# Taking VectorE instructions with two SBUF operands out of an eight-layer hybrid network on one core

## The chip, the cores and the metric

The kernel runs on one core of one Trainium2 chip. Times are device microseconds of one launch; the kernel before took 1440.38 us (median of 3 runs, 1433.18 to 1441.21). The profile is one further execution, recorded by the hardware profiler.

## The reference

A sequence of T = 2048 tokens of width 128, in f32, goes through eight residual layers, each fed the layernorm of x (`x = x + f(layernorm(x))`):

```python
x = x + L0_attn_a(ln(x))   # delta rule, 16 heads of 8: state += clip(0.9 k (v - k.state)), o = clip(state q)
x = x + L0_ffn(ln(x))      # softmax router, 2 of 8 experts + a shared one
x = x + L0_attn_b(ln(x))   # rotary, 15 largest causal logits, MLP on the keys' Gram matrix, palette sampling
x = x + L0_ffn(ln(x))
x = x + L1_attn_a(ln(x))   # linear attention, 16 heads of 8
x = x + L1_ffn(ln(x))      # sigmoid router, 2 of 8 experts + a shared one
x = x + L1_attn_b(ln(x))   # decaying linear attention, 16 heads of 8
x = x + L1_ffn(ln(x))
```

The first layer is a recurrence over all tokens. The palette layer picks 15 earlier keys for each token, gathers them, runs a small MLP, turns its output into a position on a 16 x 16 palette and a softmax weight per key, and samples the palette bilinearly. The softmax router takes the two largest of eight probabilities, the sigmoid router the two largest of `scores + bias`, weighted by the plain scores.

## The kernel before

The 16 tiles of 128 tokens are cut into nine groups, `TILES = [1, 2, 2, 2, 2, 2, 2, 2, 1]`. For each group the program writes down `delta_prepare` (queries, keys, values of the first layer), `delta_chain` (the recurrence), `delta_output`, and then `layers`: softmax router and experts (`softmax_ffn`), `palette_keys`, `palette_select`, `palette_mlp`, `palette_sample`, and the later layers. Stages are named "prepare", "chain", "output", "feed 1", "keys", "select", "network", "sample", "feed 2", "linear", "feed 3", "decay", "feed 4".

Nothing of this is issued as it is written. `Recorder` (line 37) keeps every operation, works out who needs whom, and `arrange` (line 527) then places them all in one order with costs for each operation (`cost`, line 344). Where several operations could start on an engine, the one with the smallest key goes first: its place in the program less the lead of its stage and group in the table `LEADS` (line 46). All engines get their instructions from line 636, so the profile names nearly everything L636, and tiles have to tell them apart. The scheduler also counts a port that GpSimd and those VectorE instructions share that read and write SBUF alone (`port`, line 405). In gaps of TensorE it puts filler matmuls on `zeros` (line 626); they compute nothing that is used.

Buffers are shared: `tw*` hold 128 x 256 f32, `t2k*`, `t4k*` and `t8k*` are wider. Five PSUM banks (`bank`) serve everything but the chain, which has `da_state` and two `da_coef`. When the chain is over its buffers are lent to the others, so names such as `da_ke`, `da_ks`, `da_rows`, `da_outs` and `da_kb` then stand for other work.

The chain runs over 256 blocks of 8 tokens. A block has four scans on VectorE (`da_outs<-da_rows,da_coef`), after each some products into `da_rows`, a transpose (`da_dT`), a matmul into `da_state`, a mask on VectorE (`da_sm`), a matmul into `da_coef` and a subtraction into `da_rows` for the block after next; GpSimd makes `da_prod` two blocks ahead.

The places the change touches:

- `normed_T`: statistics on VectorE, `rstd` by two GpSimd instructions, then `shift = -mean * rstd` (tile `ln_nb`) by one VectorE instruction, then ScalarE applies both. It runs 72 times.
- `top2`: for 64 tiles in 36 calls, VectorE finds the eight largest of eight (`t2_mx`) and their places (`t2_ix`, in the profile `t_ix`), casts two places (`t_ixf`), compares them with 0 to 7 (`t_oh`), adds the two one-hots (`t_hot`); the caller multiplies with the weights (`ff_wd`, `mf_cf`).
- `softmax_ffn`: bias added out of PSUM into `ff_lg`, maximum, subtraction, exponential, sum, reciprocal, scaling; all but the exponential on VectorE, all in SBUF.
- `sigmoid_ffn`: ScalarE writes the scores to SBUF (`mf_sc`), VectorE adds the bias (`mf_bs`).
- `palette_keys`: four GpSimd products and two VectorE sums for the rotary embedding, a square on ScalarE, a sum and a bound on VectorE (`b_ss`).
- `palette_select`: after the largest 15 are found, three VectorE instructions make the distances `b_df`. Then 15 GpSimd gathers per tile read `b_table`.
- `palette_sample`: softmax weights (`b_wk`, `b_tot`), positions (`b_f`), differences to 0..15 in x and y (128 x 480), tents by two ScalarE instructions, one weighted tent (`b_wy`, 128 x 240), then GpSimd's four products of 960 (`t4kA`) and VectorE's sums.
- `delta_prepare`, `delta_output`, `delta_project`, `decay_attention`: a bound, a running maximum (`da_peak`), a clamp and a decay factor.

Of the kernel before, what the change touches and what calls it, by code (L numbers as in the profile page):

```python
# [18 lines left out]
P = 128  # L19
T = 2048  # L20
# [13 lines left out]
LOWEST = -3.0e38  # L34


class Recorder:
# [6 lines left out]
    FULL = 3500  # L44

    LEADS = {
        "prepare": [685, 1641, 2227, 1637, 932, 723, -140, 947, 2240],
        "chain": [3059, 2806, 2732, 2807, 2881, 2963, 2807, 2787, 3818],
        "output": [-231, -1175, 343, -231, -1136, -815, -1408, -3037, 36],
        "feed 1": [-869, -836, -732, -888, -1239, -1948, -2920, 423, 428],  # L50
        "keys": [-839, 8778, 2817, 2921, 2750, 3260, 2756, -75, 7010],
        "select": [261, -2380, -1879, -2588, -2788, -7871, -2344, -5168, -5908],
        "network": [1694, 1836, 1022, 924, 258, 711, 3372, 2137, 88],
        "sample": [6673, 4807, 6996, 2241, 409, 4927, 2879, 483, 4943],
        "feed 2": [453, -812, 880, 533, -787, 838, 1841, -5585, -2829],
        "linear": [-375, -875, -795, 500, 1267, -1260, -755, 29, -921],
        "feed 3": [317, -219, 715, 7152, 6750, -382, -1957, -1707, -769],
        "decay": [-1757, -1097, -1119, -1867, -1575, -1798, -8825, -2837, -4500],
        "feed 4": [-2273, -2252, -2310, -3252, -3143, -2535, -6364, -6239, -8229],
# [284 lines left out]
    def cost(self, op, writes, reads):  # L344
# [26 lines left out]
        if e == "ACT":  # L371
            gelu = self.table(op) == self.TABLES["Gelu"]
            busy = 0.07 + n * (1.0e-3 if gelu else 0.8e-3)
            done = busy + 0.1
            if isinstance(kw.get("scale"), (self.View, bass.AP)):
                busy, done = busy + 0.12, done + 0.12
            if isinstance(kw.get("bias"), (self.View, bass.AP)):
                done += 0.09
            return busy, done
# [66 lines left out]
    def fill(self, begin):  # L446


        if self.filler is None or self.filler["quiet"].buf["slot"] is None:
            return []  # L450
        while self.recent and self.recent[0][0] < begin - self.WINDOW:
            self.recent.pop(0)
        lack = self.FULL - sum(c for _, c in self.recent)
        out = []
        quiet, n = self.filler["quiet"], self.filler["columns"]
        while lack > 0 and len(out) < 8:
            t0, where = max(self.load_free, self.stream_end - 0.05), None
            q = quiet.buf
            if q["slot"] is not None and not self.pending and q["kind"]["to_go"]:
                t0, where = max(t0, q["end"]), quiet  # L460
            free = [s for s in self.kinds["bank"]["slots"] if s["buf"] is None and s["free"] <= begin]
            if free:
                f = min(free, key=lambda f: f["free"])
                t1 = max(self.load_free, self.stream_end - 0.05, f["free"])
                if where is None or t1 < t0:
                    t0 = t1
                    where = self.kinds["bank"]["tiles"][self.kinds["bank"]["slots"].index(f)]
            one = n / 2.4e3 / self.rate(t0)
            if where is None or t0 + one > begin + (0.15 if not out and lack > 0.25 * self.FULL else 0.0):
                break  # L470
            end = self.run(t0, 1, 0.045, n / 2.4e3, n)
            if where is not quiet:
                f["free"] = end + 0.05
            out.append((t0, where))
            lack -= n
        return out
# [163 lines left out]
def hybrid_kernel(ctx: ExitStack, tc: tile.TileContext, ins: dict, out: bass.AP):  # L640
# [84 lines left out]
    nc.gpsimd.memset(mhalf, -0.5)  # L725
    ones = keep([P, W], "ones", F32)
# [8 lines left out]
    def normed_T(g):  # L735
# [8 lines left out]
        for j in range(n):  # L744
            nc.vector.bn_aggr(out=mv[:, j, :], in_=st[:, j, :])
        nc.gpsimd.tensor_scalar(rstd, mv[:, :, 1], 1e-5, None, ALU.add)
        nc.gpsimd.tensor_tensor(rstd, rstd, mhalf[:, :n], ALU.pow)
        shift = small([P, W // P], "ln_nb")[:, :n]
        nc.vector.scalar_tensor_tensor(
            out=shift, in0=mv[:, :, 0], scalar=-1.0, in1=rstd, op0=ALU.mult, op1=ALU.mult  # L750
        )
# [48 lines left out]
    def top2(vals):  # L800
# [3 lines left out]
        ix = small([P, W // P, E], "t2_ix", U32)[:, :n]  # L804
        ixf = small([P, W // P, 2], "t2_ixf")[:, :n]
        oh = small([P, 2, W // P, E], "t2_oh")[:, :, :n]
        hot = small([P, W // P, E], "t2_hot")[:, :n]
        for j in range(n):
            nc.vector.max(out=mx[:, j, :], in_=vals[:, j, :])
            nc.vector.max_index(out=ix[:, j, :], in_max=mx[:, j, :], in_values=vals[:, j, :])  # L810
        nc.vector.tensor_copy(ixf, ix[:, :, 0:2])
        for s in range(2):
            nc.vector.tensor_tensor(
                oh[:, s],
                i8.unsqueeze(1).to_broadcast([P, n, E]),
                ixf[:, :, s : s + 1].to_broadcast([P, n, E]),
                ALU.is_equal,
            )
        nc.vector.tensor_tensor(hot, oh[:, 0], oh[:, 1], ALU.add)
        return hot  # L820

# [15 lines left out]
    peak = keep([P, 1], "da_peak")  # L844
    carry = keep([P, HD], "da_carry")
# [8 lines left out]
    nc.vector.memset(peak, 0.0)  # L854
# [54 lines left out]
    def delta_prepare(g):  # L909
# [9 lines left out]
        pa = bank("da_aps")[:, :NP]  # L919
# [3 lines left out]
        nc.scalar.activation(lo, pa, AF.Abs, scale=0.9)  # L923
        nc.vector.tensor_scalar(lo, lo, TINY, 2.0 * TINY, ALU.is_lt, ALU.mult)
# [176 lines left out]
    def delta_output(g):  # L1101
# [6 lines left out]
        pm = small([P, HD], "da_pm")  # L1108
# [17 lines left out]
        mx = small([P, 1], "da_mx")  # L1126
        nc.vector.tensor_reduce(out=mx, in_=pm, axis=AX.X, op=ALU.max)
        nc.vector.tensor_tensor(peak, peak, mx, ALU.max)
        delta_project(g, po)

    def delta_project(g, po):

        o = tw("da_o", TILES[g] * P)
        nc.vector.tensor_scalar(o, po, 0.9, -1.0, ALU.mult, ALU.max)
        nc.vector.tensor_scalar(o, o, 1.0, None, ALU.min)
# [66 lines left out]
    def softmax_ffn(g):  # L1202
# [4 lines left out]
        mx = small([P, W // P], "ff_mx")[:, :n]  # L1207
        tot = small([P, W // P], "ff_tot")[:, :n]
        nc.vector.tensor_tensor(lg, pl, w("f_gbias").unsqueeze(1).to_broadcast([P, n, E]), ALU.add)
        nc.vector.tensor_reduce(out=mx, in_=lg, axis=AX.X, op=ALU.max)  # L1210
        nc.vector.tensor_tensor(lg, lg, mx.unsqueeze(2).to_broadcast([P, n, E]), ALU.subtract)
        nc.scalar.activation(lg, lg, AF.Exp)
        nc.vector.tensor_reduce(out=tot, in_=lg, axis=AX.X, op=ALU.add)
        nc.vector.reciprocal(tot, tot)
        nc.vector.tensor_tensor(lg, lg, tot.unsqueeze(2).to_broadcast([P, n, E]), ALU.mult)
        wd = small([P, W // P, E], "ff_wd")[:, :n]
        nc.vector.tensor_tensor(wd, top2(lg), lg, ALU.mult)
# [50 lines left out]

    def palette_keys(g):
# [10 lines left out]
        for key in (False, True):  # L1280
# [10 lines left out]
            for lo, a, b, op in ((0, cs, sn, ALU.subtract), (half, sn, cs, ALU.add)):  # L1291
# [3 lines left out]
                nc.vector.tensor_tensor(r[:, :, lo : lo + half], tt[:, 0], tt[:, 1], op)  # L1295
            sq = tw("b_sq", n * P).rearrange("p (j c) -> p j c", c=P)
            nc.scalar.activation(sq, r, AF.Square)
            ss = small([P, W // P], "b_ss")[:, :n]
            nc.vector.tensor_reduce(out=ss, in_=sq, axis=AX.X, op=ALU.add)
            nc.vector.tensor_scalar(ss, ss, 1e-24, None, ALU.max)  # L1300
            nc.gpsimd.tensor_tensor(ss, ss, mhalf[:, :n], ALU.pow)
            rn = tw("b_rn", n * P).rearrange("p (j c) -> p j c", c=P)
# [12 lines left out]
    def palette_select(g, i, IT, InT):  # L1315
# [23 lines left out]
        nc.vector.tensor_copy(df, ix[:, :TOPK])  # L1339
        nc.vector.tensor_scalar(df, df, w("tpos")[:, i : i + 1], -1.0 / T, ALU.subtract, ALU.mult)  # L1340
        nc.vector.tensor_scalar(df, df, 0.0, None, ALU.max)
# [82 lines left out]
    def palette_sample(zb, xt):  # L1424
# [4 lines left out]
        nc.scalar.activation(wk, zb[:, 2, :], AF.Exp, bias=mx, scale=1.0)  # L1429
        nc.vector.tensor_reduce(out=tot, in_=wk, axis=AX.X, op=ALU.add)  # L1430
        nc.vector.reciprocal(tot, tot)
        nc.vector.tensor_scalar(wk, wk, tot, None, ALU.mult)
        f = small([P, 2, TOPK], "b_f")
        nc.scalar.activation(f, zb[:, 0:2, :], AF.Tanh)
        nc.vector.tensor_scalar(f, f, 1.0, 0.5 * (PAL - 1), ALU.add, ALU.mult)
        nc.vector.tensor_scalar(f, f, 0.0, float(PAL - 1), ALU.max, ALU.min)
# [4 lines left out]
        nc.vector.tensor_tensor(  # L1441
            hat, f.unsqueeze(2).to_broadcast(shape),
            w("i16").unsqueeze(1).unsqueeze(3).to_broadcast(shape), ALU.subtract,
# [4 lines left out]
        nc.vector.tensor_tensor(wy, hat[:, 1], wk.unsqueeze(1).to_broadcast([P, PAL, TOPK]), ALU.mult)  # L1448
# [24 lines left out]
        nc.vector.tensor_tensor(xt, xt, py, ALU.add)  # L1473
# [64 lines left out]
    def sigmoid_ffn(g):  # L1538
        xn, xnT = normed_T(g)
        nt, n = TILES[g], TILES[g] * P  # L1540
        sc = small([P, W // P, E], "mf_sc")[:, :nt]
        nc.scalar.activation(sc, router_logits("mf_l", xnT, w("m_gate")), AF.Sigmoid)
# [3 lines left out]
        nc.vector.tensor_tensor(cf, top2(bs), sc, ALU.mult)  # L1546
# [53 lines left out]
    def decay_attention(g):  # L1600
# [13 lines left out]
        nc.scalar.activation(lam, project("de_l", cs, w("d_w2")), AF.Sigmoid, bias=w("d_b2"), scale=1.0)  # L1614
        nc.scalar.activation(lam, lam, AF.Identity, bias=base, scale=fifth)
        nc.vector.tensor_scalar(lam, lam, 0.0, 0.9995, ALU.max, ALU.min)
# [68 lines left out]

    nc.vector.tensor_scalar(peak, peak, CAP - 2.01, None, ALU.is_gt)
# [134 lines left out]
```

## Time and profile before

| | us |
|---|---|
| median of the runs | 1440.38 |
| the profiled execution | 1444.89 |
| its span, first to last instruction | 1442.6 |
| busy: scans of the chain (`da_outs`) | 220.3 |
| gathers `b_table` | 208.2 + 23.8 |
| loads of ScalarE's tables (105) | 134.7 |
| filler matmuls (456 in program order) | 139.8 |

In the profile PE is TensorE's matmuls, PEld its weight loads, DVE is VectorE, ACT is ScalarE, POOL is GpSimd and SP issues DMAs. A row of a group reads: line, engine, operation, written tile <- read tiles, shapes, count | busy us, mean ns of one | idle time of the engine ahead of them and what ended it. Tiles that differ in number alone share a name. A row of a tile's own view gives the shortest, median and longest instruction in ns. A row of windows gives the window, its length, and per engine the busy us with the number of instructions, then the granted TensorE clock as a share of full speed, and the DMA share and rate.

```profile
q0 software_dynamic: 7936, 16.47, 4.5%
q1 hardware_dynamic: 30713, 10.36, 2.9%
HBM read 24.24 MB, written 3.27 MB: 19 GB/s over the span
```

DMA queues (packets, MB, share of 16 engines) : none takes more than 4.5%.

### The profile page before, as it was taken

The page shows a single profiled execution, that of the slowest core. Times are in us where ns is not written, and L with a number is a line of the kernel's source. Part 1 is how long each engine was busy: PE and PEld are TensorE (multiplying, and loading weights), DVE is VectorE, ACT ScalarE, POOL GpSimd, SP SyncE. Part 2 cuts the span into 40 slices and gives each one's busy share as a digit, 9 for nine tenths or more (in the row PEclk, how much of TensorE's full clock was granted, in tenths as well). Part 3 has the DMA queues.
Part 4 walks back from the last instruction along what each step waited for, and adds up shares of the span by engine and source line. Part 5 has one row for each costly group of instructions (what it writes and reads, how often), then busy time and mean ns, then how long its engine had stood idle before and what let it go on. Part 6 is the DMA issues. An engine that isn't in the chain of part 4 may idle for free.

```text
span 1442.6 us, 24150 instructions
## 1 busy us (share of the span) xinstructions
PE 1262.0 (87%) x7034; PEld 901.9 (63%) x7034; DVE 1127.2 (78%) x5192; ACT 818.5 (57%) x2029; POOL 871.4 (60%) x1233
## 2 busy tenths in 40 slices
PE   4898989898989999998989989898989898888886
PEld 3475667676566667775766657665766565445664
DVE  4788698987897689778997788988887766847733
ACT  4132244436553586577654846485557876576575
POOL 3226153557478657774876647676786758775723
PEclk9876697958898699789997989999889999899989
DMA  5001000001001000110001000010011001100000
GB/s 147 25 6 31 8 1 6 11 25 40 2 11 40 21 2 7 30 38 3 7 21 27 24 3 1 27 37 10 4 32 33 0 1 34 39 22 1 1 5 9
DMA packets 38791, 28.46 MB, mean 20 GB/s; under 512 B 21222, under 2 KB 34081, under 8 KB 38649
## 3 DMA queue, kind: packets, MB, share of 16 engines
q0 software_dynamic: 7936, 16.47, 4.5%
q1 hardware_dynamic: 30713, 10.36, 2.9%
q8 instruction: 58, 0.95, 0.3%
q14 instruction: 84, 0.69, 0.2%
HBM read 24.24 MB, written 3.27 MB: 19 GB/s over the span
## 4 chain that ended last, share of the span: by engine, by line
PE 40%; DVE 27%; POOL 14%; ACT 10%; issue 5%; DMA 3%; SPq 1%; POOLq 0%; DVEq 0%; ACTq 0%
PE bank L636 29%; PE da_coef L636 7%; POOL t2kA L636 5%; DVE da_rows L636 5%; DVE da_outs L636 5%; PE da_state L636 3%; ACT twS L636 3%; POOL t4kA L636 2%; DVE twD L636 2%; ACT t2kS L636 2%; DMA t2kA<-b_table,b_ix 2%; DVE t2kA L636 2%; DVE da_sm L636 2%; ACT t2kA L636 1%; POOL da_kb L636 1%
## 5 line engine op out<-in xcount | busy, mean ns | idle before, releaser
L636 POOL DMA_INDIRECT t2kA<-b_table,b_ix x215 | 208.2, 968 | 76.2 <-issue 47.0
L636 DVE TENSOR_TENSOR_SCAN da_outs<-da_rows,da_coef 128x30 f32<-128x30 f32 (+3 forms) x1024 | 220.3, 215 | 12.6
L636 DVE TENSOR_TENSOR da_rows<-da_coef,da_outs 128x16 f32<-128x16 f32 (+6 forms) x1116 | 186.7, 174 | 13.2
L636 POOL TENSOR_TENSOR da_prod<-da_kl,da_ke 128x112 f32<-128x112 f32 (+2 forms) x264 | 92.7, 371 | 163.4 <-PE da_coef L636 158.7
L636 ACT ACT_TABLE_LOAD x105 | 134.7, 1283 | 4.1 <-PE bank L636 1.7
L636 POOL TENSOR_TENSOR t4kA<-t2kA,t2kA 128x960 f32<-128x960 f32 x56 | 114.6, 2074 | 34.8 <-DVE t2kA L636 16.7
L636 PEld LDWEIGHTS da_coef<-da_kl,da_sm 128*128 128x128 f32 x508 | 93.9, 222 | 64.9 <-DVE da_sm L636 38.7
L636 PEld LDWEIGHTS da_state<-da_dT,da_kb 128*128 128x128 f32 x512 | 104.9, 225 | 41.0 <-DVE da_dT L636 22.1
L636 POOL TENSOR_TENSOR twS<-twS,twS 128x256 f32<-128x256 f32 (+1 forms) x119 | 79.8, 682 | 62.3 <-ACT de_last L636 35.7
L636 PE MATMUL da_coef<-da_prod,ones_blk 128*128 128x224 f32 x256 | 90.0, 438 | 25.4 <-DVE da_rows L636 17.5
L636 PE MATMUL da_coef<-da_kl,da_sm 128*128 128x8 f32 x508 | 97.5, 265 | 14.7 <-DVE da_sm L636 13.4
L636 PE MATMUL da_state<-da_dT,da_kb 128*128 128x32 f32 x512 | 98.4, 277 | 10.7 <-DVE da_dT L636 8.9
L636 DVE TENSOR_TENSOR da_sm<-da_state,ones_blk 128x128 f32<-128x128 f32 x254 | 70.9, 279 | 40.8 <-PE da_state L636 39.5
L636 ACT ACTIVATE twS<-bank 88x512 bf16<-88x512 f32 (+3 forms) x151 | 72.5, 510 | 19.8 <-PE bank L636 19.5
L636 ACT ACTIVATE t2kA<-t2kA 128x480 f32<-128x480 f32 x90 | 53.5, 601 | 52.0 <-DVE t2kA L636 50.4
L636 PE MATMUL bank<-ident,t2kA 128*128 128x128 f32 x230 | 58.9, 331 | 27.2 <-DMA t2kA<-b_table,b_ix 17.3
L636 DVE TENSOR_REDUCE t2kA<-t4kA 128x64 f32<-128x960 f32 x64 | 73.0, 1142 | 12.4 <-POOL t4kA L636 6.8
L626 PE MATMUL da_state<-zeros 128*128 128x480 bf16 x252 | 77.3, 390 | 1.3 <-DVE da_sm L636 1.2
L636 PEld LDWEIGHTS da_coef<-da_prod,ones_blk 128*128 128x128 f32 x256 | 46.1, 219 | 51.5 <-DVE da_rows L636 28.8
L636 PEld LDWEIGHTS bank<-ones_blk,twS 128*128 128x128 f32 x376 | 63.9, 231 | 21.6 <-POOL twS L636 18.9
L636 PE MATMUL bank<-ones_blk,twS 128*128 128x16 f32 x376 | 67.0, 287 | 11.4 <-POOL twS L636 10.6
L636 PEld LDWEIGHTS <-t2kS 88*128 88x128 bf16 (+1 forms) x696 | 49.4, 106 | 36.6 <-ACT t2kS L636 24.2
(727 smaller groups left out, 3669.7 us busy)
## 6 DMA issues: line engine op xcount, KB each, us to landing
da_kb<-da_ktok SPq DMA_DIRECT2D x256, 4.0 KB
t2kA<-b_table,b_ix POOLq DMA_INDIRECT x215
x<-in_x SPq DMA_DIRECT2D x7, 128.0 KB
da_ktok<-twD SPq DMA_DIRECT2D x7, 128.0 KB
out_x<-x SPq DMA_DIRECT2D x7, 128.0 KB
b_table<-twA SPq DMA_DIRECT2D x6, 128.0 KB
f_w<-in_f_w SPq DMA_DIRECT2D x1, 512.0 KB
l_wv<-in_l_wv SPq DMA_DIRECT2D x1, 512.0 KB
```

The source lines that it names most:

```text
L626: self.nc.tensor.matmul(at, lhsT=real(f["zeros"])[:, :P], rhs=real(f["zeros"]), start=not sums, stop=True, skip_group_check=True,)
L636: getattr(getattr(self.nc, o["proxy"]), o["method"])(*args, **kw)
```

## The change

The edits take VectorE instructions away whose operands all lie in SBUF. Some vanish, some become one instruction with an operand in PSUM, some go to GpSimd or ScalarE. VectorE has 503 instructions fewer in the program (5082 to 4579), GpSimd 235 more (1232 to 1467), ScalarE 118 more (2031 to 2149), TensorE 33 fillers more.

- layernorm: the shift is two GpSimd products, one of them ahead of the power.
- top two: the two largest values go to a buffer whose other six places hold a value that never occurs; `match_replace` marks them with `LOWEST`, and one instruction compares and multiplies with weights that lie in PSUM.
- routers: exponentials and sigmoid scores stay in the logits' PSUM bank; ScalarE's exponential subtracts the maximum by its bias and sums by `accum_out`.
- rotary sums, bound of the key norms, differences of the tents and the weighted tent on GpSimd; the squares are summed by ScalarE.
- distances by one ScalarE instruction; positions by one; the palette weights are divided by their sum where the result is added to x.
- the running maximum is taken once over all groups; clamp, bound and decay factor pass through PSUM.
- the scheduler: a new `LEADS` table, new filler limits, and a cost for `accum_out`.

```diff
-    FULL = 3500
+    FULL, SLACK, LACK = 3513, 0.164, 0.201
...
-        "chain": [3059, 2806, 2732, 2807, 2881, 2963, 2807, 2787, 3818],
+        "chain": [1338, 3115, 3102, 3264, 2879, 3103, 3070, 2881, 928],
...
+            if "accum_out" in kw:
+                busy, done = busy + 0.06, done + 0.15
...
         nc.gpsimd.tensor_scalar(rstd, mv[:, :, 1], 1e-5, None, ALU.add)
+        nc.gpsimd.tensor_tensor(shift, mv[:, :, 0], mone[:, :n], ALU.mult)
         nc.gpsimd.tensor_tensor(rstd, rstd, mhalf[:, :n], ALU.pow)
-        nc.vector.scalar_tensor_tensor(
-            out=shift, in0=mv[:, :, 0], scalar=-1.0, in1=rstd, op0=ALU.mult, op1=ALU.mult
-        )
+        nc.gpsimd.tensor_tensor(shift, shift, rstd, ALU.mult)
...
-    def top2(vals):
+    def top2(vals, mx, weight, to):
+        n = vals.shape[1]
+        two = needles[turns[0] % len(needles)][:, :n]
+        turns[0] += 1
+        rest = small([P, W // P, E], "t2_rest")[:, :n]
+        nc.scalar.copy(two[:, :, 0:2], mx[:, :, 0:2])
+        for j in range(n):
+            nc.vector.match_replace(
+                out=rest[:, j, :], in_to_replace=two[:, j, :], in_values=vals[:, j, :], imm_value=LOWEST
+            )
+        nc.vector.scalar_tensor_tensor(
+            out=to, in0=rest, scalar=LOWEST, in1=weight, op0=ALU.is_equal, op1=ALU.mult
+        )
...
-            nc.vector.max_index(out=ix[:, j, :], in_max=mx[:, j, :], in_values=vals[:, j, :])
-        nc.vector.tensor_copy(ixf, ix[:, :, 0:2])
...
-        nc.vector.tensor_tensor(hot, oh[:, 0], oh[:, 1], ALU.add)
...
-        nc.scalar.activation(lo, pa, AF.Abs, scale=0.9)
-        nc.vector.tensor_scalar(lo, lo, TINY, 2.0 * TINY, ALU.is_lt, ALU.mult)
+        nc.scalar.activation(size, pa, AF.Abs, scale=0.9)
+        nc.vector.tensor_scalar(lo, size, TINY, 2.0 * TINY, ALU.is_lt, ALU.mult)
...
-        nc.vector.tensor_scalar(o, po, 0.9, -1.0, ALU.mult, ALU.max)
-        nc.vector.tensor_scalar(o, o, 1.0, None, ALU.min)
+        nc.vector.tensor_scalar(po, po, 0.9, -1.0, ALU.mult, ALU.max)
+        nc.vector.tensor_scalar(o, po, 1.0, None, ALU.min)
...
-        nc.vector.tensor_reduce(out=mx, in_=lg, axis=AX.X, op=ALU.max)
-        nc.vector.tensor_tensor(lg, lg, mx.unsqueeze(2).to_broadcast([P, n, E]), ALU.subtract)
-        nc.scalar.activation(lg, lg, AF.Exp)
-        nc.vector.tensor_reduce(out=tot, in_=lg, axis=AX.X, op=ALU.add)
+        mx = largest(lg)
+        nc.scalar.mul(neg, mx[:, :, 0], -1.0)
+        for j in range(n):
+            nc.scalar.activation(
+                pl[:, j, :], lg[:, j, :], AF.Exp, bias=neg[:, j : j + 1], scale=1.0, accum_out=tot[:, j : j + 1]
+            )
         nc.vector.reciprocal(tot, tot)
-        nc.vector.tensor_tensor(lg, lg, tot.unsqueeze(2).to_broadcast([P, n, E]), ALU.mult)
+        nc.vector.tensor_tensor(pl, pl, tot.unsqueeze(2).to_broadcast([P, n, E]), ALU.mult)
...
-        nc.vector.tensor_tensor(wd, top2(lg), lg, ALU.mult)
+        top2(lg, mx, pl, wd)
...
-                nc.vector.tensor_tensor(r[:, :, lo : lo + half], tt[:, 0], tt[:, 1], op)
-            nc.scalar.activation(sq, r, AF.Square)
-            nc.vector.tensor_reduce(out=ss, in_=sq, axis=AX.X, op=ALU.add)
-            nc.vector.tensor_scalar(ss, ss, 1e-24, None, ALU.max)
+                nc.gpsimd.tensor_tensor(r[:, :, lo : lo + half], tt[:, 0], tt[:, 1], op)
+            for j in range(n):
+                nc.scalar.activation(rn[:, j, :], r[:, j, :], AF.Square, accum_out=ss[:, j : j + 1])
+            nc.gpsimd.tensor_scalar(ss, ss, 1e-24, None, ALU.max)
...
-        nc.vector.tensor_copy(df, ix[:, :TOPK])
-        nc.vector.tensor_scalar(df, df, w("tpos")[:, i : i + 1], -1.0 / T, ALU.subtract, ALU.mult)
-        nc.vector.tensor_scalar(df, df, 0.0, None, ALU.max)
+        nc.scalar.activation(df, ix[:, :TOPK], AF.Relu, bias=later[:, i : i + 1], scale=-1.0 / T)
...
-        nc.scalar.activation(wk, zb[:, 2, :], AF.Exp, bias=mx, scale=1.0)
-        nc.vector.tensor_reduce(out=tot, in_=wk, axis=AX.X, op=ALU.add)
+        nc.scalar.activation(wk, zb[:, 2, :], AF.Exp, bias=mx, scale=1.0, accum_out=tot)
-        nc.vector.tensor_scalar(wk, wk, tot, None, ALU.mult)
-        nc.vector.tensor_scalar(f, f, 1.0, 0.5 * (PAL - 1), ALU.add, ALU.mult)
-        nc.vector.tensor_scalar(f, f, 0.0, float(PAL - 1), ALU.max, ALU.min)
+        nc.scalar.activation(f, f, AF.Copy, scale=0.5 * (PAL - 1))
-        nc.vector.tensor_tensor(
+        nc.gpsimd.tensor_tensor(
             hat, f.unsqueeze(2).to_broadcast(shape),
-            w("i16").unsqueeze(1).unsqueeze(3).to_broadcast(shape), ALU.subtract,
+            centre.unsqueeze(1).unsqueeze(3).to_broadcast(shape), ALU.subtract,
         )
-        nc.vector.tensor_tensor(wy, hat[:, 1], wk.unsqueeze(1).to_broadcast([P, PAL, TOPK]), ALU.mult)
+        nc.gpsimd.tensor_tensor(wy, hat[:, 1], wk.unsqueeze(1).to_broadcast([P, PAL, TOPK]), ALU.mult)
-        nc.vector.tensor_tensor(xt, xt, py, ALU.add)
+        nc.vector.scalar_tensor_tensor(out=xt, in0=py, scalar=tot, in1=xt, op0=ALU.mult, op1=ALU.add)
...
-        nc.scalar.activation(sc, router_logits("mf_l", xnT, w("m_gate")), AF.Sigmoid)
+        sc = router_logits("mf_l", xnT, w("m_gate"))
+        nc.scalar.activation(sc, sc, AF.Sigmoid)
-        nc.vector.tensor_tensor(cf, top2(bs), sc, ALU.mult)
+        top2(bs, largest(bs), sc, cf)
...
-        nc.scalar.activation(lam, project("de_l", cs, w("d_w2")), AF.Sigmoid, bias=w("d_b2"), scale=1.0)
-        nc.scalar.activation(lam, lam, AF.Identity, bias=base, scale=fifth)
-        nc.vector.tensor_scalar(lam, lam, 0.0, 0.9995, ALU.max, ALU.min)
+        pt = project("de_l", cs, w("d_w2"))
+        nc.scalar.activation(pt, pt, AF.Sigmoid, bias=w("d_b2"), scale=1.0)
+        nc.scalar.activation(pt, pt, AF.Identity, bias=base, scale=fifth)
+        nc.vector.tensor_scalar(lam, pt, 0.0, 0.9995, ALU.max, ALU.min)
```

## The prediction

> **What bounds the kernel now.** The page first: busy shares, then the chain of waits by engine.
>
> ```profile
> PE 1262.0 (87%) x7034; PEld 901.9 (63%) x7034; DVE 1127.2 (78%) x5192; ACT 818.5 (57%) x2029; POOL 871.4 (60%) x1233
> ...
> PE 40%; DVE 27%; POOL 14%; ACT 10%; issue 5%; DMA 3%; SPq 1%; POOLq 0%; DVEq 0%; ACTq 0%
> ```
>
> No engine is the bound over the whole span: the path changes hands between TensorE and VectorE. So I cut the span by the last scan of the delta chain, which the trace shows at 1100 us, and by 320 us, when side work fills up.
>
> ```profile
> 0.00:320.00 320.00, 269.34 (x1246) 197.02 (x1247) 259.92 (x1498) 114.40 (x339) 135.51 (x270) 0.79 0.11 29
> 320.00:1100.00 780.00, 701.78 (x4017) 511.97 (x4017) 652.99 (x3092) 474.78 (x1145) 528.79 (x716) 0.90 0.08 19
> 1100.00:1443.00 343.00, 290.84 (x1776) 192.88 (x1775) 214.25 (x604) 229.28 (x546) 207.06 (x249) 0.93 0.05 13
> ```
>
> Columns: window, then busy us of PE, PEld, DVE, ACT, POOL, then granted clock. From 320 to 1100 VectorE is 0.84 busy. TensorE is 0.90 busy, but 53 us of that are the filler matmuls on `zeros` (same windows for that tile), so its real work is 649/780 = 0.83. The chain is not at its own floor there: 16 blocks of it take 44 us between 71.5 and 115.9 us, where little else runs, and 75 to 80 us later. It queues behind side work on VectorE. After 1100 VectorE is 0.62 busy: that stretch runs on the latency of the last groups.
>
> Next, what VectorE's side work costs. The router tile shows it (min/median/max ns):
>
> ```profile
> L636 DVE TENSOR_TENSOR ff_lg<-ff_lg,ff_mx x18: 143/166/1865, 99.4 to 1329.8; 128x16 f32<-128x16 f32 x14, 128x8 f32<-128x8 f32 x4
> L636 DVE TENSOR_TENSOR ff_lg<-ff_lg,ff_tot x18: 140/168/2566, 103.4 to 1331.4; 128x16 f32<-128x16 f32 x14, 128x8 f32<-128x8 f32 x4
> L636 DVE TENSOR_TENSOR ff_lg<-bank,f_gbias x17: 139/164/175, 98.9 to 1329.4; 128x16 f32<-128x16 f32 x13, 128x8 f32<-128x8 f32 x4
> ```
>
> Same shape, same work: with one operand in PSUM the worst takes 175 ns, with both in SBUF the worst takes 2566 ns. The timeline tells why:
>
> ```profile
> 1417.51 1.90 POOL L636 TENSOR_TENSOR da_rows<-da_ke,mf_cf 128x1024 bf16<-128x1024 f32 x1 [0.75 <-DVE mf_cf L636]
> 1419.36 1.90 POOL L636 TENSOR_TENSOR t2kS<-da_ke,mf_cf 128x1024 bf16<-128x1024 f32 x1
> ...
> 1417.86 1.57 DVE L636 CAST t_ixf<-t_ix 128x2 f32<-128x2 uint32 x1
> 1419.46 1.89 DVE L636 TENSOR_TENSOR t_oh<-i,t_ixf 128x8 f32<-128x8 f32 x2
> ```
>
> A two-element cast takes 1.57 us and ends with a GpSimd instruction, and the pair behind it lasts as long as the next one. GpSimd and SBUF-only VectorE work exclude each other, and VectorE's whole queue waits, the chain included.
>
> **What is removed from VectorE.** From the rows by form, busy us: top two: casts 8.2 + 2.9, one-hots 7.8 + 4.0 (14.5 as a plain sum, since neighbours overlap), sums of them 5.6 + 1.3; weight products 9.0, softmax maximum, subtraction, sum and scaling 16.7, router bias 4.2; the layernorm shift 18.5 (72 instructions); rotary sums 12.9; key norms 9.4; distances 11.4; sampling 30.1 (b_f 6.6, the 480-wide difference 10.4, the 240-wide product 6.5, sum and scale 6.7); the running peak 3.4. Plain sum 148 us in 578 instructions: 18 before 320 us, 75 to 1100, 55 after. In their place come 72 instructions with a PSUM operand (scaling, weights, bias) at the 0.163 us of the row above, 11.7 us, and 64 match-replaces for 64 index searches: at equal width both cost the same (2274 and 2284 ns at 2048), so nothing. Net 136 us: 16, 69 and 51.
>
> The clamp's second half and the decay factor now read PSUM. The row from SBUF is 321 ns at 256 elements, the one from PSUM 413: about 1 us in all, which I drop. The Trainium skill (VectorE: DVE Perf Modes, section Why PSUM operands drop a tier) speaks against these edits, since a PSUM operand costs an instruction its doubled rate. The rows agree for wide tiles, while for 16 elements the two rows differ by 4 ns at the median; by the rule alone this would lose 1 to 2 us and the stalls would not count.
>
> **What GpSimd takes.** These are the nearest rows:
>
> ```profile
> L636 POOL TENSOR_TENSOR twA<-twA,b_cos 128x128 f32<-128x128 f32 x25 | 11.5, 470 | 1.8 <-ACT twA L636 1.8
> L636 POOL TENSOR_TENSOR t2kA<-t2kA,t2kA 128x512 f32<-128x512 f32 x16 | 20.6, 1294 | 9.5 <-issue 6.7 <-ACT t2kA L636 2.7
> L636 POOL TENSOR_SCALAR ln_rstd<-ln_mv 128x2 f32<-128x2 f32 x56 | 12.7, 226 | 60.4 <-DVE ln_mv L636 36.5 <-DVE da_rows L636 10.4 <-DVE ln_nb L636 7.3
> ```
>
> Two tiny products per norm are 144 at between 0.1 us (a two-element memset took 123 ns) and 0.226; I take 0.2, near the arithmetic row: 29 us. Rotary sums 28 x 0.45 + 8 x 0.32 = 15; key norms 18 x 0.226 = 4; tents 16 x 1.21 (1294 x 480/512) = 19 and 16 x 0.70 = 11. Sum 79 us, so POOL goes from 871 to 950. It works in order: behind these wait the gathers `b_table` (240 at 0.97 us, 93 us of the chain of waits) and the chain's `da_prod`, which idled 159 us for PE and so has room. The Trainium skill (GPSIMD Engine Reference, section 4.1 Engine selection) advises VectorE for elementwise work, GpSimd being about twice as slow; by it the moved 32 us would cost 65 instead of the 50 of the rows, 15 us more on GpSimd.
>
> **ScalarE and TensorE.** ScalarE gains 36 needle copies and 18 negations at 0.19, 14 exponentials, 16 distances and 16 tent scalings at 0.21, three table loads at 1.283, and squares by tile: 27 us on an engine with 43% idle. The accumulators have no row; between nothing and the 0.16 of the reduction they replace, I take 0.06. Off the path: nothing. Fillers go from 456 to 489 in program order, 33 x 0.39 = 13 us in gaps. Keeping the router in PSUM holds a bank longer: from the bias to the weights 222 us over 18 calls, from sigmoid to weights 142 over 18, against 5 x 1443 of banks, 5%. TensorE's longest waits are for operands (`da_sm`, `da_rows`, `t2kS`), none for a freed bank: nothing, and up to 10 us if banks run short.
>
> **What of it shows.** Two bounds. By the path: walking the chain of waits piece by piece, the leaving instructions hold 42 us of it (7, 26, 9 by window). What stays on the path elsewhere: rotary 8.4 us at 470/405 is 9.8, tents 4.6 at 1294/650 x 480/512 is 8.6, the shift's last product about 5, the rest 4. Net gain 15. By VectorE's load: 16 + 69 before 1100, and 4 after (9 less half), 89. Between them TensorE limits: its real 649 us fit into no less than 729 at 0.89 (the stretch 480 to 640 ran at 0.94, and some 0.05 of filler stays), so 51 instead of 69, in sum 71. Neither row is nearer: I take 50, about midway between 15 and 89. The profiled execution took 1444.9 us (span 1442.6), 0.3% over the median 1440.4. 1444.9 - 50 is 1395, and against the median 1390: I say **1392 us**.
>
> The issue order shows where it goes. At the last chain scan 195 of 240 gathers stand issued before the change, 165 after. The chain will end earlier, about 1000 us, and the tail grows from 343 to some 390.
>
> **Rivals.** VectorE was alone in the way: 89 us and the stalls' knock-on, 1350 (1335 to 1365). For it: 0.84 busy, and stalls of up to 2.6 us in its queue. Against it: PE on 40% of the path.
> TensorE or the banks are late at once: 15 us less 10, 1432. For it: 0.83 real load, `da_sm` and `da_rows` waiting 74 us for PE. Here too belongs that the change does not do what it says, because stalls remain on other SBUF-only work.
> GpSimd becomes the bound, the slower side: in the stretch where gathers, tents and products meet (1180 to 1260, POOL 0.76 busy, 0.40 of it gathers). If its queue passes about 0.9 there and in the selects before, half or more of the 79 us lie on the path: 1444.9 + 45 - 15, 1475. It decides once gathers wait for tents instead of for indices.
>
> **How the numbers follow.** The forecast 0.55 (1365 to 1425), VectorE alone 0.16, TensorE or banks 0.17, GpSimd 0.12. About 1% is what a measurement of this kernel can tell from no change. Faster by more: 0.55 + 0.16 = 0.71; within it 0.17; slower 0.12. The range 1348 to 1445 leaves out the lower half of the second case, 0.08, and the last, 0.12.
>
> **What would show it.** VectorE near 990 us busy and 4580 instructions, no VectorE instruction of 16 elements over 0.4 us; the last scan near 1000 us; POOL near 950; TensorE above 0.90 from 320 to the chain's end. Wrong if POOL's share of the chain passes 20%, if PE waits for banks, or if GpSimd's tiny products cost 0.4 us or more.

## The result, and the profile after

The kernel after takes 1448.45 us (median of 20 runs, 1435.80 to 1457.16) against 1441.80 us for the kernel before in the same job (20 runs): a ratio of 1.0066, 95% interval 1.0036 to 1.0095. The change makes the kernel 0.7% slower, some 10 us. The ratio compares fast runs alone, leaving out those of the kernel before that took over 1.5% more than its fastest; the medians of all runs give 1.0046. The profiled execution took 1454.08 us, span 1452.3, at a granted clock of 0.871, the lowest of the 20 runs (median 0.888).

The busy shares on the page of the kernel after:

```profile
PE 1281.8 (88%) x7067; PEld 909.2 (63%) x7067; DVE 1055.7 (73%) x4689; ACT 843.2 (58%) x2227; POOL 934.6 (64%) x1468
```

VectorE is busy 71.5 us less (1127.2 to 1055.7), GpSimd 63.2 us more, ScalarE 24.7 us more. The work was moved rather than removed: what left VectorE is only 71.5 us, while the rows of its instructions, summed one by one, fell by 129 us (1432.8 to 1303.7). Neighbours in VectorE's queue overlap (1432.8 us of rows fit into 1127.2 us before), so a row's 160 ns is not 160 ns of the engine. (The page's chain of waits breaks off after an eighth of this span and is not read here.)

The same execution by windows, columns as before (PE, PEld, DVE, ACT, POOL busy, then granted clock):

```profile
0.00:320.00 320.00, 262.64 (x1239) 181.76 (x1239) 232.78 (x1268) 115.81 (x342) 129.25 (x291) 0.82 0.10 26
320.00:1100.00 780.00, 711.28 (x3960) 518.38 (x3958) 634.11 (x2941) 476.85 (x1240) 552.42 (x838) 0.87 0.07 19
1100.00:1452.00 352.00, 307.92 (x1873) 209.03 (x1872) 188.83 (x482) 250.59 (x646) 252.96 (x341) 0.91 0.05 15
```

From 320 to 1100 us VectorE went from 0.84 to 0.81 busy, TensorE from 0.90 to 0.91. The last scan of the chain ends at 1068 us instead of 1101, and what follows it takes 384 us instead of 342. A lower clock of TensorE is not what made the kernel slower: its runs have a median of 0.888, the kernel before 0.876 to 0.880 in five of the six sets below.

The stalls are gone. The router tile again (min/median/max ns), and the compare pair that now follows the maximum:

```profile
L639 DVE MATCH_VALUE_LOAD t_rest<-needles,ff_lg x32: 58/81/92, 97.2 to 1333.4; 128x8 f32 x32
L639 DVE MATCH_REPLACE8 t_rest<-needles,ff_lg x32: 148/151/154, 97.3 to 1333.4; 128x8 f32<-128x8 f32 x32
L639 DVE TENSOR_TENSOR ff_lg<-bank,f_gbias x16: 130/171/178, 93.4 to 1332.0; 128x16 f32<-128x16 f32 x12, 128x8 f32<-128x8 f32 x4
```

Where the worst was 2566 ns, no VectorE row of this tile is above 178 ns. Over all of VectorE, what single instructions took beyond the median of their own tile and form, counted where it was more than a fifth, came to 37.1 us before (22.4 of it after 1100 us) and to 0.3 us after. The Trainium skill (VectorE: DVE Perf Modes, section Two Vector instructions with no wait between them) says that what an instruction with two SBUF inputs reads second goes through an interface shared with GpSimd; these two figures agree with it. The cast shown ahead, which stalled for 1.57 us, has one input, so two are not needed for a stall.

What ScalarE and GpSimd got, by form (busy us, mean ns):

```profile
L639 ACT ACTIVATE bank<-ff_lg,ff_neg 128x8 f32<-128x8 f32 x28 | 7.6, 270 | 0.3
L639 ACT ACTIVATION_READ_ACCUMULATOR bank<-ff_lg,ff_neg 128x1 f32 x28 | 5.3, 190 | 0.0
L639 ACT ACTIVATION_READ_ACCUMULATOR twA<-twA 128x1 f32 x28 | 5.3, 188 | 0.0
```

```profile
L639 POOL TENSOR_TENSOR t2kA<-b_f,b_centre 128x480 f32<-128x480 f32 x13 | 13.2, 1018 | 27.3 <-ACT b_f L639 26.4 <-ACT de_last L639 0.9
L639 POOL TENSOR_TENSOR ln_nb<-ln_nb,ln_rstd 128x2 f32<-128x2 f32 x56 | 10.8, 192 | 1.7
L639 POOL TENSOR_TENSOR t2kA<-t2kA,b_wk 128x240 f32<-128x240 f32 x10 | 6.5, 647 | 10.5 <-ACT t2kA L639 7.0 <-DVE twD L639 1.7 <-ACT da_carry L639 1.6
```

GpSimd's prices are as forecast or a little lower (1018 ns where 1210 was taken, 192 where 200 was). ScalarE's accumulator is an instruction of its own of 188 to 190 ns, 80 in all.

And the new order has a hole. VectorE's timeline between two scans of the chain:

```profile
243.86 0.23 DVE L639 TENSOR_TENSOR_SCAN da_outs<-da_rows,da_coef 128x36 f32<-128x36 f32 x1
...
245.59 0.29 DVE L639 TENSOR_TENSOR x<-x,bank 128x128 f32<-128x128 f32 x1
...
274.21 0.42 DVE L639 TENSOR_REDUCE da_peaks<-twD 128x1 f32<-128x64 f32 x2
...
297.61 0.17 DVE L639 TENSOR_TENSOR da_rows<-da_vl,da_coef 128x8 f32<-128x8 f32 x1 [0.33 <-PE da_coef L639]
297.81 0.22 DVE L639 TENSOR_TENSOR_SCAN da_outs<-da_rows,da_coef 128x30 f32<-128x30 f32 x1
```

The chain stands for 54 us; before, its longest pause from the start of one scan to the start of the next was 11.5 us. The scans after the hole are those of group 2's last three blocks, and what goes ahead of them already reads group 3's keys (`da_prod` at 296.46 us). So they need `delta_prepare(3)`, whose bounds are ready at 295.5 us instead of 221. It comes behind group 1's output (`da_peaks` at 274), which comes behind the late layers of group 0 (its tile of x goes out at 275 us instead of 354): the new `LEADS` put them in that order. So the first theory of the miss was this hole; the second, that each us that GpSimd and ScalarE got costs as much as one on VectorE is worth; the third, that TensorE is late next.

### The profile page after: what moved, and what is told of

The parts are those of the page before. It is cut to its first block, busy times and chain, and to the rows that moved or that the text cites. A ratio compares the mean times of both kernels' runs of the same rounds, so it can differ in the third digit from the quotient of the medians.

```text
span 1452.3 us, 24233 instructions
## 1 busy us (share of the span) xinstructions
PE 1281.8 (88%) x7067; PEld 909.2 (63%) x7067; DVE 1055.7 (73%) x4689; ACT 843.2 (58%) x2227; POOL 934.6 (64%) x1468
## 5 line engine op out<-in xcount | busy, mean ns | idle before, releaser
L639 POOL DMA_INDIRECT t2kA<-b_table,b_ix x218 | 211.3, 969 | 66.0 <-issue 48.6
L639 POOL TENSOR_TENSOR twS<-twS,twS 128x256 f32<-128x256 f32 (+1 forms) x121 | 80.5, 676 | 37.7 <-ACT de_last L639 22.4
L639 DVE TENSOR_TENSOR da_sm<-da_state,ones_blk 128x128 f32<-128x128 f32 x254 | 71.5, 282 | 45.1 <-PE da_state L639 42.1
L629 PE MATMUL da_state<-zeros 128*128 128x480 bf16 x308 | 102.2, 418 | 1.5 <-DVE da_sm L639 1.5
L639 POOL TENSOR_TENSOR t4kA<-t2kA,t2kA 128x960 f32<-128x960 f32 x40 | 81.9, 2073 | 5.4 <-DVE t2kA L639 4.9
L629 PEld LDWEIGHTS <-zeros 128*128 128x128 bf16 x488 | 64.0, 142 | 24.7 <-issue 12.3
L639 PEld LDWEIGHTS bank<-ones_blk,twS 128*128 128x128 f32 x380 | 58.4, 213 | 25.8 <-POOL twS L639 21.4
L639 ACT ACTIVATE twS<-bank 88x512 bf16<-88x512 f32 (+4 forms) x136 | 64.6, 502 | 14.7 <-PE bank L639 13.8
L639 PE MATMUL bank<-ones_blk,twS 128*128 128x16 f32 x380 | 61.5, 274 | 11.7 <-POOL twS L639 10.4
L639 DVE TENSOR_TENSOR da_rows<-da_vl,da_coef 128x8 f32<-128x8 f32 x254 | 40.7, 160 | 38.0 <-PE da_coef L639 37.1
L639 ACT ACTIVATE t2kA<-t2kA 128x480 f32<-128x480 f32 x79 | 47.3, 601 | 33.7 <-DVE t2kA L639 31.9
L639 PEld LDWEIGHTS bank<-t8kA 128*128 128x128 f32 x400 | 55.9, 220 | 16.0 <-issue 9.0
```

Source lines behind the costliest of these rows:

```text
L629: self.nc.tensor.matmul(at, lhsT=real(f["zeros"])[:, :P], rhs=real(f["zeros"]), start=not sums, stop=True, skip_group_check=True,)
L639: getattr(getattr(self.nc, o["proxy"]), o["method"])(*args, **kw)
```

## The experiments

The runs came in six sets, and ratios are against the kernel before in the same set. There it took 1442 to 1444 us, and 1498 us in the second set alone (the three kernels of which the middle one doubles ScalarE's work). The kernel after was in none of the sets: where a kernel is compared with it, its 1.0066 is meant, and such a difference is uncertain by about 0.5% (7 us), by up to 0.8% where few runs were made. "Order held" means that the scheduler places everything as in the kernel named, and an instruction is then sent to another engine, sent twice, or left out at its place:

```diff
-            return lambda *a, **k: self.rec.add(self.name, method, a, k)
+            return lambda *a, **k: self.rec.add(self.name, method, a, k, self.goes, self.times)
...
-            getattr(getattr(self.nc, o["proxy"]), o["method"])(*args, **kw)
+            for _ in range(o["times"]):
+                getattr(getattr(self.nc, o["proxy"]), o["method"])(*args, **kw)
...
-                nc.vector.tensor_tensor(r[:, :, lo : lo + half], tt[:, 0], tt[:, 1], op)
+                nc.other.tensor_tensor(r[:, :, lo : lo + half], tt[:, 0], tt[:, 1], op)
```

The last pair is the pattern for each instruction that an expectation names; `other` carries the engine and the number of times (2 or 3, 0 where it is left out, and then a buffer that nobody writes any more is set once at the start).

**Moving and doubling.** The rotary sums and tents in the kernel before sent to GpSimd:

> The kernel before, its written order held; only the rotary sums (36) and the two tent instructions (32) are issued on GpSimd in place of VectorE, at the places in the order that they had. VectorE loses 29.8 us (12.9 + 16.9 in its rows), GpSimd gains about 41.5 us (the rows of the kernel after). Theory 'price of VectorE' (the prediction: about 0.37 us of time per us of VectorE): 1432, 10 us faster. Theory 'GpSimd takes the place': 1455 or more. Theory 'the order sets the time': within 8 us of the kernel before, since the order and with it every stall of the chain is the same.

Measured 1.0061 (1.0014 to 1.0107): 9 us slower. The same instructions of the kernel after sent back to VectorE:

> The kernel after, its written order held; the same 68 instructions go back to VectorE in place. VectorE +30 us, GpSimd -42 us. Price of VectorE: 1459. GpSimd takes the place: 1425 to 1435. The order sets the time: 1440 to 1456, with the stall of the chain of about 54 us near 244 us still there.

1.0123 (1.0050 to 1.0197) where the kernel after has 1.0066; the hole is still there, 48.8 us. Moved off the engine that the order was made for, they cost some 8 us either way (the second figure is within its uncertainty): the price of VectorE forecast the second and not the first, GpSimd's the first, about, and not the second. The theory of the order had both within 1 us of its bounds. Then the same instructions sent twice:

> The kernel after, its order held; the same 68 instructions are issued twice on GpSimd (+42 us there, nothing else). If GpSimd is on the path in the selects and the tail: 1470 to 1490, half of the 42 us or more. If it is not: 1448 to 1456. The price of GpSimd that comes out is what its +63 us of the change can have cost.

1.0298 (1.0222 to 1.0375): 33 us more than the kernel after (22 to 45), for 41 us more on GpSimd (934.6 to 976.0 busy).

> The kernel before, its order held; the same 68 instructions are issued twice on VectorE (+30 us there). Price of VectorE of 0.37: 1453. If VectorE's load is no bound by itself: 1442 to 1446. If it is the bound from 320 us to the chain's end: 1465 or more.

1.0206 (1.0133 to 1.0279): 30 us (19 to 40) for 31 us more on VectorE (1127.2 to 1157.9). Work added to either engine costs nearly all of its length. Is that so for the small instructions too, and on ScalarE?

> The kernel after, its order held; the first of GpSimd's two tiny products of each layernorm is issued three times (144 more instructions at 0.192 us, 27.6 us on GpSimd, nothing else). If every us on GpSimd costs a us (the tents and rotary sums issued twice cost 39 us for 42): 1475. If only what lies in the selects costs: 1450 to 1456.

1.0367 (1.0295 to 1.0438), 3.0% above the ratio of the kernel after, 45 us of that set for 28 us on GpSimd.

> The kernel after, its order held; what the change gave ScalarE is issued twice: needle copies, negations, the exponentials and squares with their accumulator reads, the distances (about 200 instructions; by the rows some 45 us, since an accumulator read is an instruction of its own of 188 ns). The prediction took ScalarE to be off the path: 1448 to 1453. If ScalarE's instructions lie in the same chains of steps as the others: 1470 to 1490.

1.0408 (1.0331 to 1.0485), 51 us for 38 us on ScalarE (843.2 to 881.5). Added work on ScalarE isn't free either. In the slower set these two differences are rougher still.

> The kernel before, its order held; the small VectorE instructions that the change removes are issued twice where that gives the same result: index searches, casts, one-hots and their sums, softmax maximum and sum, weight products, layernorm shifts (352 instructions, 58 us by the medians of their rows, 76 with the stalls). Plain sum as load (the prediction's way of counting): 1495 or more. Only the time between issues counts (the union of busy time fell by 71 us where the plain sum fell by 129): 1470 to 1480. Side work that hides: 1442 to 1450.

1.0451 (1.0368 to 1.0535), 68 us for 60 us more busy time (1127.2 to 1187.1). All five say that added work costs 0.8 to 1.6 us per busy us, on whichever engine. In each the granted clock is lower too (medians 0.838 to 0.866, where the same kernel without the added work, or the kernel before in that set, has 0.860 to 0.888), so a part of the price may come by way of TensorE's clock; that was not separated. They say nothing yet of what work taken away returns.

**Taking away, order held.**

> The kernel before, its order held; the two tent instructions of each tile (the 480-wide difference and the 240-wide product, 32 instructions, 16.9 us on VectorE) are left out, so the sampling weights are not computed. Issued twice together with the rotary sums, these cost 31 us for 30. If taking away is worth what adding costs: 1425. If a removed instruction only uncovers what is late next: 1434 to 1444.

1.0020 (0.9976 to 1.0064): nothing came back. But VectorE's busy time fell by 5.7 us only (1127.2 to 1121.5), since stalls moved to other instructions whose operands lie in SBUF. The scaling of the weights, in the kernel before and here (the longest one here runs from 835.37 to 837.44 us, beside a GpSimd product into `t4kA` from 835.36 to 837.41):

```profile
L636 DVE TENSOR_SCALAR b_wk<-b_wk,b_tot x16: 206/224/780, 183.0 to 1304.0; 128x15 f32<-128x15 f32 x16
L638 DVE TENSOR_SCALAR b_wk<-b_wk,b_tot x16: 206/229/2073, 182.9 to 1307.9; 128x15 f32<-128x15 f32 x16
```

> The kernel after, its order held; the same 32 instructions, now 26.6 us on GpSimd, are left out, so the sampling weights are not computed. If taking away is worth what adding costs on GpSimd (0.8 us per us): 1430, that is 0.992 of the kernel before. If it only uncovers what is late next: 1440 to 1448, 1.000 to 1.006.

1.0013 (0.9974 to 1.0052): 8 us less than the kernel after (1 to 15), a third of the 24 us by which GpSimd's busy time fell. Leaving out these instructions returned less than adding work had cost. With so few us at stake the larger case decides:

> The kernel before, its order held; VectorE is relieved of 348 of the small instructions that the change removes, 90.8 us as a plain sum of their rows (index searches 14.9, casts 11.1, one-hots 14.5, their sums 6.9, softmax maximum and subtraction 8.0, layernorm shifts 18.5, tents 16.8), and no other engine gets anything. What they compute is left out: the two chosen experts, the subtraction of the maximum, the layernorm shift, the sampling weights. Prediction's price (0.37): 1408. A price of 1 on the stalls and the busy time (half of the plain sum): 1395. Late next (TensorE and the hops between engines hold the order's pace, nothing comes of it): 1430 to 1444.

0.9871 (0.9825 to 0.9917), 19 us faster (12 to 25), between the prediction's price (1408) and "late next" (1430 to 1444). Its page, and the middle window:

```profile
PE 1254.2 (88%) x7034; PEld 900.0 (63%) x7034; DVE 1076.4 (76%) x4780; ACT 814.6 (57%) x2029; POOL 870.9 (61%) x1239
```

```profile
320.00:1100.00 780.00, 707.04 (x4066) 515.52 (x4066) 641.67 (x2878) 480.26 (x1162) 531.74 (x720) 0.90 0.07 19
```

The rows named in the expectation, 90.8 us, are 50.8 us of busy time, and these return 19 us: 0.21 us per us of rows, 0.37 per busy us (0.24 to 0.50). What VectorE then waits for, in the kernel before, in this one and in the kernel after (us in total, times, longest):

```profile
DVE x L636 <- PE bank L636: 39.7, 22, 10.3
DVE da_sm L636 <- PE da_state L636: 39.5, 38, 5.0
```

```profile
DVE da_sm L641 <- PE da_state L641: 49.0, 43, 5.3
DVE x L641 <- PE bank L641: 48.7, 24, 14.7
```

```profile
DVE x L639 <- PE bank L639: 61.1, 27, 12.0
DVE da_sm L639 <- PE da_state L639: 42.1, 43, 3.9
```

The relieved VectorE waits longer for TensorE: the two rows grow from 79 to 98 and 103 us. That TensorE is what comes late next is read from these waits; no run shows it apart.

> The kernel after, its order held; GpSimd is relieved of both tiny products of each layernorm (144, 27.5 us) and of the tents (32, 26.7 us), so that its busy time falls to about that of before. The layernorm shift and the sampling weights are left out. GpSimd took VectorE's place as the bound: 1405 to 1420, 0.975 to 0.985 of the kernel before. Late next: 1435 to 1445, 0.995 to 1.002.

0.9997 (0.9958 to 1.0036): 10 us less than the kernel after (3 to 17), for 47 us of busy time (934.6 to 887.7). GpSimd is not the bound; the hole in the chain is still there (51.8 us).

**TensorE.** The filler matmuls left out:

```diff
                 sums = isinstance(o, self.View)
+                continue
                 f = self.filler
```

> The kernel before, its order held, without its 456 filler matmuls (177.6 us on TensorE, on zeros: nothing is left out of the result). If TensorE's busy time is the bound: faster, 1400. If its granted clock sets the pace (0.884 in the kernel before): the clock falls and the time grows by at least as much, 1500 or more at a clock of 0.8. If neither: within 10 us.

1.0504 (1.0444 to 1.0563). The page:

```profile
PE 1279.3 (85%) x6579; PEld 982.0 (66%) x6579; DVE 1132.5 (76%) x5192; ACT 821.4 (55%) x2029; POOL 873.1 (58%) x1233
```

The granted clock falls from 0.884 to 0.803 in the profiles (0.877 to 0.769 by the medians of this set), and the other matmuls, which by their records are busy for 1170 us in the kernel before (fillers overlap with them), now take 1279 us. By the medians, 12% less clock goes with 5% more time: the clock is a part of what sets the pace, not all of it. The Trainium skill (TensorE: Matmul & The Clock Gate, section HAM oscillation) says that pauses longer than about 3.4 us put the array back to half its clock. This trace shows that such pauses are not needed: the longest between two matmul records (their ends are modelled) is 3.35 us, and still the granted clock was half of the full one for 593 of 1499 us.

**The order.** The instructions of the kernel after in another order, and the same treatment of the kernel before. A list gives each instruction a time; nothing is released more than 7 or 8 us ahead of the earliest one left:

```diff
-        return self.arrange(self.priorities(self.LEADS))
...
+        keys, at, raw = [], 0, zlib.decompress(base64.b85decode(ORDER))
+        for i in range(0, len(raw), 4):
+            at += int.from_bytes(raw[i : i + 4], "little", signed=True)
+            keys.append(1e-4 * at)
...
+            upto = keys[line[head]] + ahead + more
...
+                    if keys[i] > upto:
+                        continue
```

> The instructions of the kernel after, unchanged, in another order: each takes the place in time that it (or what it depends on) had in the order of the kernel before, and the 117 places of the stages and groups are then shifted by a few us; group 1's output again comes before group 0's last layers, so the 54 us stall of the chain near 244 us is gone. It also has more fillers. If the stall is what ate the gain (theory 'order'): 1395 to 1415, and the chain's end near 1030. If the us that left VectorE are paid for on GpSimd and ScalarE (theory 'each us counts on every engine'): the order found is worth 10 to 25 us, 1420 to 1435, and the same treatment gives the kernel before as much.

0.9915 (0.9864 to 0.9966): 12 us faster than before, 22 us faster than the kernel after, and the only version that computes everything and beats both. By windows:

```profile
0.00:320.00 320.00, 266.72 (x1424) 182.18 (x1425) 259.12 (x1463) 124.65 (x382) 158.00 (x340) 0.93 0.12 30
320.00:1100.00 780.00, 704.63 (x4060) 507.01 (x4057) 618.77 (x2785) 486.77 (x1265) 560.13 (x825) 0.92 0.08 19
```

The hole is gone (longest pause 11.6 us), the chain ends at 1086, the rest takes 346 us, and the clock is 0.93 and 0.92 in place of 0.82 and 0.87. (By the medians of the runs it is 0.927 in place of 0.888, with 612 fillers in place of 489.)

> The control: the instructions of the kernel before, the places of their stages and groups shifted in the same manner and with the same effort, with more fillers too. Theory 'order': 1425 to 1442, clearly behind the kernel after in its new order. Theory 'each us counts on every engine': 1415 to 1435, the two within 10 us of each other.

1.0286 (1.0236 to 1.0337), 41 us slower, against both expectations: shifts chosen by the scheduler's own costs can end well or badly on the chip. With the same instructions but for the fillers (646 in place of 456), another order moves the time by 3%, several times what this change did; its granted clock is no lower (0.891, 0.880 in the kernel before).

> The instructions of the kernel after in the order of the kernel before: each is released at the place in time that it (or what it depends on) had there, within 7 us, with no shifts and with the filler thresholds of the kernel after. It undoes the reordering that came with the change and nothing else. If the stall of the chain and the new order cost the gain: 1425 or less, the 54 us stall gone. If the new order was needed to make the new instructions fit: 1450 to 1475.

1.0186 (1.0132 to 1.0240), as the second theory had it. The hole is gone (longest pause 11.5 us), and the kernel is slower still: its chain ends at 1116 us, its clock is 0.863 (median), with 481 fillers. So the hole alone did not eat the gain. What, then, earned the 1.5% of the new order, its places or its 612 fillers? Every fifth filler is left out of it, or every fourth (third) of a kernel's own is sent twice:

```diff
+                count += 1
+                if count % 5 == 0:
+                    continue
```

> The kernel after in its new order (0.9915 of before), with every fifth of its 612 filler matmuls left out, so that 490 remain as in the kernel after (489). If the order earned the 1.5%: 0.990 to 0.996 of before. If the fillers did, by the granted clock (0.919 there, 0.871 in the profile of after): the clock falls to about 0.88 and the ratio returns to 1.003 to 1.010.

1.0078 (1.0041 to 1.0114), clock 0.891: without every fifth filler the whole gain is gone.

> The kernel after in its own order, with every fourth of its 489 filler matmuls issued twice (611, as in the new order). If fillers earned the gain: clock 0.90 or more, 0.990 to 0.998 of before. If the order did: 1.005 to 1.015, since a filler more stands in TensorE's queue before real work.

1.0058 (1.0025 to 1.0090), clock 0.896: as many fillers, doubled in place, give the kernel after nothing.

> The kernel before in its own order, with every third of its 456 filler matmuls issued twice (608). If TensorE's granted clock can still be raised with a gain (taking all fillers away cost 5%): 0.985 to 0.995. If it is already as high as pays: 1.000 to 1.015.

1.0014 (0.9985 to 1.0043): nor the kernel before. Fillers paid only in the order that was planned with them; the gain belongs to the two together. With as many fillers as the kernel after, left out evenly and not by a plan, the order without the hole is no faster than the one with it (1.0078 against 1.0066).

## Why the prediction was wrong

Foreseen were 1392 us, within 1348 to 1445, and faster by over 1% at 0.71; it came out 0.7% slower, above the range.

- **The stalls: right.** VectorE instructions with all operands in SBUF waited for GpSimd, and with them gone 37.1 us became 0.3 us. But 22 of these lay after 1100 us, where VectorE was only 0.62 busy.
- **What is removed from VectorE: mis-sized.** "Net 136 us" is a sum of rows, and as such nearly right (they fell by 129 us). But the engine lost 71.5 us of busy time, so VectorE stayed at 1056 us where 990 were foreseen. This is the first step that failed: rows of neighbours overlap, which the prediction says of the one-hots, and it summed the rest all the same. There is no fixed rate between the two, either: the copies of b_before_small_twice added 66 us of rows and 60 us of busy time.
- **What of it shows: too much.** 50 us for 136 is 0.37 per us of rows; e_before_vector_relieved returned 0.21. That it returned 0.37 per busy us is a coincidence of two different units. For the 71.5 us this is 26 us, not 50, and the other bound, 89 us (VectorE's load), was far out. VectorE was not alone in the way. TensorE's "real 649 us" from 320 to 1100 were too low as well: fillers overlap with real matmuls, and by the records these alone are busy for 669 us, 0.86 of the window (672 in the kernel after). By the prediction's own formula its third figure is then 48 us instead of 71 (an estimate).
- **What GpSimd takes: sizes right, cover wrong.** 934.6 us against 950 foreseen, tiny products 192 ns against 200. But it was not free: 47 us given back return 10 (3 to 17), so the 63 us cost about 13 by that rate.
- **ScalarE "off the path: nothing": wrong.** The load was sized about right, 24.7 us busy against 27 foreseen, though the accumulator, taken at 0.06 us, is an instruction of 188 ns, 15 us over 80. The price of nothing had no run behind it: doubling what ScalarE got cost 51 us, 1.3 per busy us; by this its 25 us cost up to 33. What leaving them out would return was not tried.
- **Fillers and banks.** 33 more fillers in gaps: doubling 122 of them in the kernel after changed nothing. That banks were held longer was not tried apart.
- **The order.** The chain was to end near 1000 us with a tail of some 390: the tail came out at 384, but the chain at 1068, after a hole of 54 us that can be read from the order of issue of the kernel after, and was not looked for. The runs do not show that the hole cost anything by itself.

Summed, as an estimate: 26 us gained, 13 lost on GpSimd, nothing to 33 on ScalarE, between 13 us faster and 20 slower; measured 10 slower. So the runs show why 50 us did not come, and by this estimate half of what did come went to GpSimd; what turned the rest into a loss, ScalarE or the new order, stays open.

Of the rivals, TensorE late at once (1432) fits best: taking work away in place (50.8 busy us, against 71.5 for the change) gave 19 us, and the wait for TensorE grew. That is support for its mechanism, not proof. It was still too fast, since it too let GpSimd and ScalarE go free. GpSimd as the bound (1475) fell: its relief gave 10 us, not 45, though it was 0.79 to 0.87 busy from 1100 to 1340 us. VectorE alone (1350) fell.

## What to carry to other kernels

Count the load that leaves an engine by its busy time, not by the sum of its instructions' durations, and price it by an experiment that leaves the work out without giving it to anyone: here an added busy us cost 0.8 to 1.6 us, a removed one returned nothing to 0.4. In this kernel, where four engines hand small tiles to each other, work moved from one to another was paid for there. And before a gain of 1% is put down to instructions, ask what another order of them, with its fillers, does: here up to 3%.

## What the hardware showed that was not expected

- An activation with an accumulator is two instructions on ScalarE, the second 188 ns long for one element per partition.
- Match-replace, too, is two: a load of the eight values (81 ns) and the pass (151 ns).
- A ninth of TensorE's busy time (139.8 of 1262 us) is matmuls on zeros. Leaving them out makes the rest take 1279 us instead of 1170, at half the clock for 593 us though no pause was longer than 3.35 us.
- A stall that is taken from one instruction can come back on another: without the tents (16.9 us of rows) VectorE was busy 5.7 us less, and the longest scaling of the weights took 2073 ns instead of 780.
